# Graph layer with gathers by edge: when the dense part's work is issued, how the first groups are normalised, and how the edge list ends

## The chip, the core and the metric

The kernel runs on one core of one Trainium2 chip. A core has five engines with queues of their own: PE (TensorE, matmuls, with PEld for its weight loads), DVE (VectorE), ACT (ScalarE), POOL (GpSimd, which here issues the gathers) and SP (SyncE, which here issues the plain DMAs). The metric is the device time of the kernel in microseconds, as the median of several runs.

## What is computed

```python
def reference(x, src, dst, edge_type_4, L0_gnn_W, L0_gnn_b):   # x: 12500 x 128, 200000 edges, 4 types
    h = jnp.maximum(_layernorm(x, axis=-1), 0.0)
    xs = h[src]
    msgs = 0
    for i in range(4):
        msgs = msgs + jnp.where((edge_type_4 == i)[:, None], xs @ W[i] + b[i], 0.0)
    return x + jax.ops.segment_sum(msgs, dst, num_segments=12500)
```

The edges are sorted by destination, and the destinations are drawn so that low node numbers have many more edges than high ones.

## The kernel before

**Chunks and groups.** The edges are cut into 1,563 chunks of 128. The first 384 chunks (three blocks of 128 chunks, `DENSE = 3`) go through a dense path; the other 1,179 are handled by gathers, in groups of `G = 16` (73 groups of 16, then one of 8 and one of 3). The loop at L658 runs over these groups. For each, `gather` (L335) issues one indirect DMA on POOL for each chunk: 128 rows, one per edge, into `hm`, whose pool `rows` has five buffers of `HG = 8` chunks each. `sum_up` (L350) then makes a one-hot matrix `oh` for each chunk on DVE (L359: key equal to column number), multiplies the rows by it on PE into `ps` (L369, which sums the rows by destination and type within a window of 16, 24 or 32 nodes), copies `ps` to `sb` on ACT (L376), counts the edges by type (`pc`, L381, copied to `cnt` by L385), multiplies by the weights of the four types and adds the biases into `py` (L387, L389), and adds each chunk's window to its place in `acc`, which holds the transposed sums of all nodes in SBUF (L399, DVE). `sum_up` is a generator: it yields after each `SG = 4` chunks' copies.

**Raw groups and the table.** The first `RAW = 8` groups gather rows of `x` and normalise them after the gather (`normalize`, L294: bn_stats and bn_aggr for each row block on DVE, a square root on ACT, a reciprocal and a product on DVE, then one activation per chunk on ACT, L309). Meanwhile `table` (L311) loads `x` in pieces of `XG = 8` node columns, normalises them in the same way, splits each value into three bfloat16 parts (L318 to L321) and writes them to `htab` in HBM. From group 8 on the gathers read `htab`, three parts a row, so L369 runs three matmuls for each chunk. `prep_edges` (L190) turns blocks of 128 x 128 edges into the transposed index table `srcT` and key table `keyT`: loads of source, type and destination, DVE arithmetic, two transposes on PE through `pt`, and copies. One block is done at the head; nine more, in calls of up to four, in groups 2 to 4. `prep_dense` (L239) runs in group 1.

**The dense path.** After group 7 `make_slots` (L474) computes for the first 792 nodes a table of 984 slots (one slot: up to 128 edges of one node). `dense_work` (L597) is a generator over 18 passes of 46 columns each. A pass first builds `counts`: for each slot two one-hots on DVE (L612, L613), one matmul on PE into `pt` (L617), and a copy on ACT (L619). Then it multiplies the whole table by the counts: 98 blocks of `htab` loaded by SP in tiles `hs` of four (L627, five buffers), three matmuls a block (L633) into `pa`. `sd` takes the sum (L642), four matmuls apply the weights (L645), and the result is added to `acc` (L650). The main loop draws dense work between the parts of `sum_up`, by cost:

```python
while work and spent < share * (gi - RAW + part):     # L715
    cost = next(work, None)
```

A slot counts 0.25, a block 0.33, and `share = total / (len(sizes) - RAW - 6)`.

**The end.** `put_out` (L402) loads a piece of `x` into `xo`, transposes that part of `acc` on PE into `pt` (L416), adds (L419) and stores (L423, L425). The pieces are 8 node columns of 128 wide, and 4 among the last ones; a piece is put out as soon as no later chunk can reach it. `check_all` (L446) prepares a flag; a slow path behind it (L750) is not taken here.

**Order.** A scheduler in the framework orders each engine's instructions from the traced program, by its own model of time: an instruction traced later can stand earlier in its engine's queue where its inputs are ready earlier in that model. Each engine then runs its queue in order. PSUM pools: `x_ps` (tiles `pt`, three buffers), `s_ps` (`ps`, three), `y_ps` (`py`, one), `a_ps` (`pa`, one).

Of the kernel before, what the change touches and what calls it, by code (L numbers as in the profile page):

```python
# [32 lines left out]
F32 = mybir.dt.float32  # L33
# [10 lines left out]
P = 128  # L44
# [10 lines left out]
OB = 4  # L55
HG = 8


@with_exitstack
def kernel(  # L60
# [107 lines left out]
    wpool = whats.enter_context(tc.tile_pool(name="what", bufs=1))  # L168
    prep = early.enter_context(tc.tile_pool(name="prep", bufs=2))
    npool = early.enter_context(tc.tile_pool(name="nodes", bufs=2))  # L170


# [14 lines left out]
    nc.vector.tensor_single_scalar(span, span, 16.0, op=ALU.add)  # L187
    QB = 4

    def prep_edges(q0, q1):  # L190
        n = q1 - q0
        m0, m1 = q0 - DENSE, q1 - DENSE
        si = prep.tile([P, QB, P], I32, name="si")
        edge_rows(si, src, q0, q1, 0)
        ty = prep.tile([P, QB, P], I32, name="ty")
        edge_rows(ty, etype, q0, q1, NT)
        di = prep.tile([P, QB, P], I32, name="di")
        edge_rows(di, dst, q0, q1, 0)
# [10 lines left out]
        (nc.scalar.copy if m0 == 0 else nc.vector.tensor_copy)(srcT[:, m0:m1, :], pg[:, :n, :])  # L209
# [21 lines left out]
    nc.scalar.copy(warm, warm)  # L231
    prep_edges(DENSE, DENSE + 1)

# [49 lines left out]
    eps = const.tile([P, 1], F32, name="eps")  # L283
    nc.vector.memset(eps, EPS)
    pick = const.tile([P, NT, N3], BF16, name="pick")
# [7 lines left out]

    def normalize(xt, h, n, r, what):  # L294

        mv = what.tile([P, G, 2], F32, name="mv")
        rstd = what.tile([P, G], F32, name="rstd")
        nmr = what.tile([P, G], F32, name="nmr")
        for k in range(n):
            st = what.tile([P, 6], F32, name="st")  # L300
            nc.vector.bn_stats(st[:r], xt(k))
            nc.vector.bn_aggr(mv[:r, k, :], st[:r])
# [3 lines left out]
            nmr[:r, :n], mv[:r, :n, 0], -1.0, rstd[:r, :n], op0=ALU.mult, op1=ALU.mult  # L306
        )
        for k in range(n):
            nc.scalar.activation(h(k), xt(k), AF.Relu, bias=nmr[:r, k : k + 1], scale=rstd[:r, k : k + 1])  # L309

    def table(j0, j1, r):  # L311
        n = j1 - j0
        xt = npool.tile([P, XG, D], F32, name="xt")
        load_nodes(xt, j0, j1)
        h = npool.tile([P, XG, D], F32, name="h")
        h3 = npool.tile([P, XG, 3, D], BF16, name="h3")
        normalize(lambda k: xt[:r, k, :], lambda k: h[:r, k, :], n, r, npool)
        nc.scalar.copy(h3[:r, :n, 0, :], h[:r, :n, :])  # L318
# [30 lines left out]

    def sum_up(t0, g, rows, raw):  # L350
        win = window_of(C0 + t0)
        K = NT * win
        if raw:
            oh = npool.tile([P, G, P], F32, name="ohf")[:, :, :K]
            normalize(lambda k: rows(k, 0, 1), lambda k: rows(k, 0, 1), g, P, npool)
        else:
            oh = opool.tile([P, G, P], BF16, name="oh")[:, :, :K]
        for i in range(g):
            nc.vector.tensor_scalar(  # L359
                oh[:, i, :], (iota_f if raw else iota_b)[:, :K], keyf[:, t0 + i : t0 + i + 1], None, ALU.is_equal  # L360
            )
        sb = spool.tile([P, G * P], F32, name="sb")[:, : G * K].rearrange("p (g t n) -> p g t n", g=G, t=NT)
        nparts = 1 if raw else 3
        for i0 in range(0, g, SG):
            i1 = min(i0 + SG, g)
            ps = s_ps.tile([P, SG, P], F32, name="ps")[:, :, :K]
            for i in range(i0, i1):
                for c in range(nparts):
                    nc.tensor.matmul(  # L369
                        ps[:, i - i0, :],  # L370
# [5 lines left out]
            nc.scalar.copy(sb[:, i0:i1].rearrange("p g t n -> p g (t n)"), ps[:, : i1 - i0, :])  # L376
            yield i1 / g
        ohv = oh.rearrange("p g (t n) -> p g t n", t=NT)
# [6 lines left out]
        nc.scalar.copy(cnt[:, :g], pc[:, :g])  # L385
        py = y_ps.tile([P, G * WIN], F32, name="py")[:, : G * win].rearrange("p (g n) -> p g n", g=G)
        nc.tensor.matmul(py[:, :g, :], b12, cnt[:, :g, :], start=True, stop=False)  # L387
# [40 lines left out]
    for j0 in range(0, NW, XG):  # L428
        for ja, jb in ((j0, min(j0 + XG, NW)),) if j0 + XG < NW - XG else ((j0, j0 + XG // 2), (j0 + XG // 2, j0 + XG)):
            jb = min(jb, NW)  # L430
            if jb > ja:
                flushes.append((ja, jb, T * (min(jb * P, N) / N) ** 0.5 + ROOM - C0))

    sizes = [G] * (TM // G)
    r = TM % G
    sizes += [r - r // 3, r // 3] if r > 3 else [r] if r else []
    starts = [sum(sizes[:i]) for i in range(len(sizes))]
# [159 lines left out]
    def dense_work():  # L597
        for v0 in range(0, len(virtual), VB):
# [8 lines left out]
            for s0 in range(0, len(todo), OB):  # L607
# [6 lines left out]
                for k, (i, s, first, last) in enumerate(part):  # L614
# [3 lines left out]
                    if last:  # L618
                        nc.scalar.copy(  # L619
                            counts[:, :, i * NT : (i + 1) * NT], pb.rearrange("p (b t) -> p b t", t=NT)  # L620
                        )
                    yield 0.25
            pa = a_ps.tile([P, VB * NT], F32, name="pa")
            for j0 in range(0, NW, HB):
# [5 lines left out]
                for j in range(j0, j1):  # L630
                    r = P
                    for c in range(3):
# [6 lines left out]
                        )  # L639
                yield 0.33 * (j1 - j0)  # L640
            sd = hsp.tile([P, VB, NT], F32, name="sd")
# [16 lines left out]
    for gi, (t0, g) in enumerate(zip(starts, sizes)):  # L658
        raw = gi < RAW
        if gi == 0:  # L660
            rows = gather(t0, g, x, D)
            for a in tables[:1]:
                table(*a)
            w3 = w.rearrange("t i o -> i t o")
# [32 lines left out]
            nc.vector.tensor_copy(b12, bs)  # L697
            for a in tables[1:2]:
                table(*a)
            done = 2  # L700
        elif raw:
            rows = gather(t0, g, x, D)
            for a in tables[done : done + 2]:
                table(*a)
            done += 2
            if gi == 1:
                prep_dense()
            elif DENSE + 1 + (gi - 2) * QB < TB:
                prep_edges(DENSE + 1 + (gi - 2) * QB, min(DENSE + 1 + (gi - 1) * QB, TB))
        else:  # L710
            rows = gather(t0, g, htab, D3)
        if gi == RAW - 1:
            assert done >= len(tables)
        for part in sum_up(t0, g, rows, raw):
            while work and spent < share * (gi - RAW + part):  # L715
                cost = next(work, None)
                if cost is None:
                    work = None
                else:
                    spent += cost  # L720
        if gi == RAW - 1:
# [5 lines left out]
            whats.close()  # L727
            outp = mid.enter_context(tc.tile_pool(name="outp", bufs=2))
            dense = mid.enter_context(tc.tile_pool(name="dense", bufs=1))
# [3 lines left out]
            total = 0.25 * NS + 0.33 * NW * -(-len(virtual) // VB)  # L733
# [136 lines left out]
```

## Time and profile before

| | |
|---|---|
| median of 3 runs | 1597.66 us (1597.22 to 1600.49) |
| the profiled execution | 1600.88 us, span in the trace 1599.2 us |
| mean granted PE clock | 0.899 |
| busy: PE, DVE, ACT, POOL | 1289.5, 931.2, 621.7, 1153.8 us |
| gathers (L341) | 128 from `x`, mean 1026 ns; 1,051 from `htab`, mean 971 ns |
| one-hot pairs of the counts (L612, L613) | 984, mean 251 and 336 ns |
| products with the table (L633) | 5,292 matmuls, 469.6 us busy |
| DMA | 318.92 MB, mean 199 GB/s |

The span runs from the first to the last instruction of the trace; the profiled execution's own time is a little longer. A matmul's duration in the trace is its latency; matmuls overlap, so the distance from start to start is what a series of them costs. The same holds for DVE instructions, whose rows overlap slightly. Idle time of an engine is put down to what ended it ("issue" is time in which the profile shows nothing that the engine waited for).

### The profile page before, as it was taken

Reading aid. Unit: us, or ns where it says so; the run is one execution under the profiler, and the core shown is the slowest. Engines: PE = TensorE matmul, PEld = TensorE weight load, DVE = VectorE, ACT = ScalarE, POOL = GpSimd, SP = SyncE. Lnnn points to the kernel's source line nnn. Section 1 sums busy time; section 2 is a strip of 40 time slices with the busy share of each in tenths; the row PEclk is TensorE's granted clock in tenths of the full one; section 3 lists DMA queues with packets and bytes.
Section 4 is the critical chain, followed back from the end, with each engine's and each line's share of the span. In section 5 each row is a group of like instructions: output and inputs, shape, how many; then the busy total and the mean of one; then the engine's idle time right before and its main releaser. Section 6 shows DMA issues by size and latency. Waiting matters only on the chain.

```text
span 1599.2 us, 33065 instructions
## 1 busy us (share of the span) xinstructions
PE 1289.5 (81%) x11086; PEld 904.8 (57%) x11086; DVE 931.2 (58%) x5157; ACT 621.7 (39%) x1505; POOL 1153.8 (72%) x1189
## 2 busy tenths in 40 slices
PE   0636577888989889886589989989899889899965
PEld 0424443465757667765366766746667567486633
DVE  8786769848494573562247366564473645648232
ACT  4756723433333353251145335153252432515110
POOL 7775577277777777777767777777777777777771
PEclk9755678998989999998599999989999999999976
DMA  6453343374748759767365876848769577595641
GB/s 177 147 163 106 97 126 98 96 253 122 277 139 285 260 180 304 264 196 262 102 216 184 306 236 197 313 143 281 237 191 316 159 266 237 186 315 165 216 118 43
DMA packets 155501, 318.92 MB, mean 199 GB/s; under 512 B 28504, under 2 KB 77834, under 8 KB 155325
## 3 DMA queue, kind: packets, MB, share of 16 engines
q1 hardware_dynamic: 100781, 204.98, 36.9%
q0 software_dynamic: 54544, 111.78, 24.3%
q8 instruction: 88, 1.44, 0.4%
q14 instruction: 88, 0.72, 0.1%
HBM read 300.62 MB, written 16.03 MB: 198 GB/s over the span
## 4 chain that ended last, share of the span: by engine, by line
PE 33%; DMA 18%; DVE 15%; POOL 13%; ACT 10%; issue 8%; DVEq 0%; POOLq 0%; ACTq 0%
DMA hs<-htab 15%; PE pa L633 13%; POOL hm L341 13%; PE py L389 7%; ACT counts L619 7%; DVE o L613 6%; DVE o L612 4%; PE ps L369 4%; PE pt L617 3%; PE ps L381 2%; DVE acc L399 2%; ACT hm L309 2%; DMA hm<-htab,srcT 2%; DMA hm<-in_x_dram,srcT 1%; PE py L645 1%
## 5 line engine op out<-in xcount | busy, mean ns | idle before, releaser
L341 POOL DMA_INDIRECT hm<-htab,srcT x1051 | 1021.0, 971 | 358.9 <-issue 290.6
L633 PE MATMUL pa<-counts,hs 128*128 128x184 bf16 x5292 | 469.6, 245 | 59.5 <-DMA hs<-htab 51.5
L633 PEld LDWEIGHTS <-hs 128*128 128x128 bf16 x5292 | 416.1, 99 | 99.1 <-DMA hs<-htab 84.4
L619 ACT CAST counts<-pt 128x392 bf16<-128x392 f32 x828 | 352.1, 535 | 123.6 <-PE pt L617 119.4
L376 ACT COPY sb<-ps 128x256 f32<-128x256 f32 (+2 forms) x295 | 128.2, 445 | 637.4 <-PE ps L369 591.7
L359 DVE TENSOR_SCALAR oh<-iota_b,keyT 128x96 bf16<-128x96 bf16 (+2 forms) x1051 | 201.9, 265 | 254.8 <-PE ps L381 254.4
L399 DVE TENSOR_TENSOR acc<-acc,py 128x16 f32 (+2 forms) x1179 | 206.2, 175 | 233.3 <-PE py L389 191.0
L617 PE MATMUL pt<-o,o 128*128 128x392 bf16 x984 | 302.5, 343 | 40.0 <-DVE o L613 14.8
L613 DVE TENSOR_SCALAR o<-iota_n,hkT 128x392 bf16<-128x392 f16 x984 | 330.8, 336 | 0.0
L612 DVE TENSOR_SCALAR o<-iota_b,loT 128x128 bf16<-128x128 bf16 x984 | 247.0, 251 | 52.5 <-PE pt L617 50.1
L369 PE MATMUL ps<-oh,hm 128*128 128x96 bf16 (+2 forms) x3153 | 209.1, 207 | 64.2 <-DMA hm<-htab,srcT 57.6
L369 PEld LDWEIGHTS <-hm 128*128 128x128 bf16 x3153 | 167.2, 100 | 126.0 <-DMA hm<-htab,srcT 76.5
L389 PE MATMUL py<-sb,wsb 128*128 128x256 f32 (+2 forms) x600 | 212.3, 484 | 0.0
L617 PEld LDWEIGHTS <-o 128*128 128x128 bf16 x984 | 96.5, 100 | 186.6 <-DVE o L613 126.2
L341 POOL DMA_INDIRECT hm<-in_x_dram,srcT x128 | 131.3, 1026 | 55.2 <-issue 35.4
L389 PEld LDWEIGHTS py<-sb,wsb 128*128 128x128 f32 x600 | 115.3, 206 | 58.8 <-issue 30.9
L369 PE MATMUL ps<-ohf,hm 128*128 128x64 f32 x256 | 58.7, 416 | 92.8 <-ACT hm L309 61.9
L369 PEld LDWEIGHTS ps<-ohf,hm 128*128 128x128 f32 x256 | 54.7, 320 | 97.9 <-ACT hm L309 90.6
L385 ACT CAST cnt<-ps 12x256 bf16<-12x256 f32 (+3 forms) x75 | 31.5, 421 | 119.0 <-PE ps L381 113.6
L381 PE MATMUL ps<-oh,pick 128*12 128x384 bf16 (+3 forms) x268 | 61.4, 330 | 0.6 <-ACT sb L376 0.6
L309 ACT ACTIVATE hm<-hm,nmr,rstd 128x128 f32<-128x128 f32 x128 | 50.2, 479 | 4.9 <-DVE nmr L305 4.9
L309 ACT ACTIVATE h<-xt,nmr,rstd 128x128 f32<-128x128 f32 x98 | 40.0, 481 | 9.0 <-DVE nmr L305 9.0
(146 smaller groups left out, 522.3 us busy)
## 6 DMA issues: line engine op xcount, KB each, us to landing
hs<-htab SPq DMA_DIRECT2D x432, 384.0 KB
hm<-htab,srcT POOLq DMA_INDIRECT x1051
htab<-h SPq DMA_DIRECT2D x11, 768.0 KB
xo<-in_x_dram SPq DMA_DIRECT2D x11, 512.0 KB
out_dram<-xo SPq DMA_DIRECT2D x11, 512.0 KB
hs<-htab SPq DMA_DIRECT2D x18, 192.0 KB
xt<-in_x_dram SPq DMA_DIRECT2D x6, 512.0 KB
xt<-in_x_dram SPq DMA_DIRECT2D x5, 448.0 KB
```

Of the source, the lines that this page charges most:

```text
L309: nc.scalar.activation(h(k), xt(k), AF.Relu, bias=nmr[:r, k : k + 1], scale=rstd[:r, k : k + 1])
L341: nc.gpsimd.indirect_dma_start(out=rows[:, (i - h0) * width : (i - h0 + 1) * width], out_offset=None, in_=table, in_offset=bass.IndirectOf ...
L359: nc.vector.tensor_scalar(oh[:, i, :], (iota_f if raw else iota_b)[:, :K], keyf[:, t0 + i : t0 + i + 1], None, ALU.is_equal)
L369: nc.tensor.matmul(ps[:, i - i0, :], rows(i, c, nparts), oh[:, i, :], start=(c == 0), stop=(c == nparts - 1),)
L376: nc.scalar.copy(sb[:, i0:i1].rearrange("p g t n -> p g (t n)"), ps[:, : i1 - i0, :])
L389: nc.tensor.matmul(py[:, :g, :], wsb[:, t, :], sb[:, :g, t, :], start=False, stop=(t == NT - 1))
L399: nc.vector.tensor_tensor(to, to, py[:, i, :], ALU.add)
L612: nc.vector.tensor_scalar(o1[:, k, :], iota_b, loT[:, s : s + 1], None, ALU.is_equal)
L613: nc.vector.tensor_scalar(o2[:, k, :], iota_n, hkT[:, s : s + 1], None, ALU.is_equal)
L617: nc.tensor.matmul(pb, o1[:, k, :], o2[:, k, :], start=first, stop=last)
L619: nc.scalar.copy(counts[:, :, i * NT : (i + 1) * NT], pb.rearrange("p (b t) -> p b t", t=NT))
L633: nc.tensor.matmul(pa[:, : nv * NT], hs[:r, j - j0, c * D : (c + 1) * D], counts[:r, j, : nv * NT], start=(j == 0 and c == 0), stop=(j == ...
```

## The change

It has seven parts.

- **The dense work starts three groups later** (`LEAD = 3`: first in group 11), is spread over 60 groups instead of 61, and is costed at 0.6 for a slot and 0.3 for a block.
- **It is tied**: `sum_up` yields the last matmul of each four chunks, and `tc.issue_after(mm)` puts every PE instruction of the dense work drawn there behind that matmul in PE's queue.
- **Table statistics a group ahead**: `look` loads a piece of `x` and computes its statistics; `table`, one group later, uses them.
- **Raw groups by halves**: the one-hots come first, then each half (8 chunks) gets its own statistics and normalisation.
- **Later keys in the loop**: only two blocks are prepared in group 3; the other seven come one at a time, at groups 16, 24, ... 64, eight groups ahead of their use.
- **Smaller last groups**: 72 groups of 16, then 12, 8, 4 and 3. From group 72 on `py` is taken from `x_ps` (tiles `pt`). The last 10 node columns are put out by twos.
- `acc` is zeroed on ACT instead of DVE, and `eps` is derived from a value that depends on the first index table.

```diff
+LEAD = 3
...
-    prep = early.enter_context(tc.tile_pool(name="prep", bufs=2))
+    prep = early.enter_context(tc.tile_pool(name="prep", bufs=1))
+    aheads = early.enter_context(tc.tile_pool(name="aheads", bufs=4))
...
-    QB = 4
-    def prep_edges(q0, q1):
+    QB = max(2, DENSE)
+    def prep_edges(q0, q1, prep, QB):
...
-        (nc.scalar.copy if m0 == 0 else nc.vector.tensor_copy)(srcT[:, m0:m1, :], pg[:, :n, :])
+        nc.scalar.copy(srcT[:, m0:m1, :], pg[:, :n, :])
...
-    nc.vector.memset(eps, EPS)
+    zero = const.tile([P, 1], F32, name="zero")
+    nc.vector.tensor_single_scalar(zero, srcT[:, 0, 0:1], 0.0, op=ALU.mult)
+    nc.vector.tensor_single_scalar(eps, zero, EPS, op=ALU.add)
...
+    def look(j0, j1, r):
+        xt = npool.tile([P, XG, D], F32, name="xt", bufs=4)
+        load_nodes(xt, j0, j1)
+        seen_x[j0] = xt, stats(lambda k: xt[:r, k, :], j1 - j0, r, aheads, "t")
...
-            normalize(lambda k: rows(k, 0, 1), lambda k: rows(k, 0, 1), g, P, npool)
...
+        if raw:
+            for h0 in range(0, g, HG):
+                row = lambda k: rows(h0 + k, 0, 1)
+                n = min(HG, g - h0)
+                normalize(row, row, n, P, stats(row, n, P, npool, ""))
...
-                    nc.tensor.matmul(
+                    mm = nc.tensor.matmul(
...
-            yield i1 / g
+            yield i1 / g, mm.ins
...
-        py = y_ps.tile([P, G * WIN], F32, name="py")
+        py = (x_ps.tile([P, G * WIN], F32, name="pt") if last else y_ps.tile([P, G * WIN], F32, name="py"))
...
+        step = XG if j0 + XG < NW - XG else 2
...
+    ends_in = [12, 8, 4, 3]
+    FULL = (TM - sum(ends_in)) // G
+    r = TM - sum(ends_in) - FULL * G
+    sizes = [G] * FULL + ([r] if r else []) + ends_in
...
-                    yield 0.25
+                    yield 0.6
...
-                yield 0.33 * (j1 - j0)
+                yield 0.3 * (j1 - j0)
...
-                nc.vector.memset(acc[:, k : min(k + NC // 8, NC)], 0.0)
+                n = min(k + NC // 8, NC) - k
+                nc.scalar.copy(acc[:, k : k + n], zero.to_broadcast([P, n]))
...
-            elif DENSE + 1 + (gi - 2) * QB < TB:
-                prep_edges(DENSE + 1 + (gi - 2) * QB, min(DENSE + 1 + (gi - 1) * QB, TB))
+            elif gi == 3:
+                prep_edges(DENSE + 1, DENSE + 3, prep, QB)
...
+            q = (t0 + 8 * G) // P
+            if (t0 + 8 * G) % P < G and DENSE + 3 <= DENSE + q < TB:
+                prep_edges(DENSE + q, DENSE + q + 1, later, 1)
...
-        for part in sum_up(t0, g, rows, raw):
-            while work and spent < share * (gi - RAW + part):
+        for part, mm in sum_up(t0, g, rows, raw, gi >= FULL):
+            with tc.issue_after(mm):
+                while work and spent < share * (gi - RAW - LEAD + part):
...
-            share = total / (len(sizes) - RAW - 6)
+            share = total / (FULL - RAW - LEAD - 1)
...
-        if gi == len(sizes) - 6:
+        if gi == FULL - 6:
             check_all()
```

More of the change, by code (lines that the diff above doesn't have):

```diff
@@ L231 @@
     nc.scalar.copy(warm, warm)
-    prep_edges(DENSE, DENSE + 1)
+    prep_edges(DENSE, DENSE + 1, prep, QB)
     first0 = const.tile([P, DENSE], F32, name="first0")
@@ L291, with stats @@
     nc.vector.tensor_copy(pick_f, pick)
[L294 to L298, printed above, removed]
+    def stats(xt, n, r, what, tag):
+        mv = what.tile([P, XG, 2], F32, name="mv" + tag)
+        rstd = what.tile([P, XG], F32, name="rstd" + tag)
+        nmr = what.tile([P, XG], F32, name="nmr" + tag)
         for k in range(n):
-            st = what.tile([P, 6], F32, name="st")
+            st = what.tile([P, 6], F32, name="st", bufs=4)
             nc.vector.bn_stats(st[:r], xt(k))
@@ L307, in normalize @@
         )
+        return rstd, nmr
+    def normalize(xt, h, n, r, of):
+        rstd, nmr = of
         for k in range(n):
             nc.scalar.activation(h(k), xt(k), AF.Relu, bias=nmr[:r, k : k + 1], scale=rstd[:r, k : k + 1])
+    seen_x = {}
+    def look(j0, j1, r):
+        xt = npool.tile([P, XG, D], F32, name="xt", bufs=4)
+        load_nodes(xt, j0, j1)
+        seen_x[j0] = xt, stats(lambda k: xt[:r, k, :], j1 - j0, r, aheads, "t")
     def table(j0, j1, r):
         n = j1 - j0
-        xt = npool.tile([P, XG, D], F32, name="xt")
-        load_nodes(xt, j0, j1)
+        xt, of = seen_x.pop(j0)
         h = npool.tile([P, XG, D], F32, name="h")
         h3 = npool.tile([P, XG, 3, D], BF16, name="h3")
-        normalize(lambda k: xt[:r, k, :], lambda k: h[:r, k, :], n, r, npool)
+        normalize(lambda k: xt[:r, k, :], lambda k: h[:r, k, :], n, r, of)
         nc.scalar.copy(h3[:r, :n, 0, :], h[:r, :n, :])
@@ L348, in gather, with sum_up @@
         return lambda i, c, n: got[i // HG][:, (i % HG * n + c) * D : (i % HG * n + c + 1) * D]
-    def sum_up(t0, g, rows, raw):
+    def sum_up(t0, g, rows, raw, last):
         win = window_of(C0 + t0)
@@ L385, in sum_up @@
         nc.scalar.copy(cnt[:, :g], pc[:, :g])
-        py = y_ps.tile([P, G * WIN], F32, name="py")[:, : G * win].rearrange("p (g n) -> p g n", g=G)
+        py = (x_ps.tile([P, G * WIN], F32, name="pt") if last else y_ps.tile([P, G * WIN], F32, name="py"))[:, : G * win].rearrange("p (g n) -> p g n", g=G)
         nc.tensor.matmul(py[:, :g, :], b12, cnt[:, :g, :], start=True, stop=False)
@@ L428 @@
     for j0 in range(0, NW, XG):
[L429 to L436, printed above, removed]
+        step = XG if j0 + XG < NW - XG else 2
+        for ja in range(j0, min(j0 + XG, NW), step):
+            jb = min(ja + step, NW)
+            flushes.append((ja, jb, T * (min(jb * P, N) / N) ** 0.5 + ROOM - C0))
+    ends_in = [12, 8, 4, 3]
+    FULL = (TM - sum(ends_in)) // G
+    r = TM - sum(ends_in) - FULL * G
+    sizes = [G] * FULL + ([r] if r else []) + ends_in
     starts = [sum(sizes[:i]) for i in range(len(sizes))]
@@ L661 @@
             rows = gather(t0, g, x, D)
-            for a in tables[:1]:
-                table(*a)
+            for a in tables[:2]:
+                look(*a)
             w3 = w.rearrange("t i o -> i t o")
@@ L697 @@
             nc.vector.tensor_copy(b12, bs)
-            for a in tables[1:2]:
+            for a in tables[:2]:
                 table(*a)
+            for a in tables[2:4]:
+                look(*a)
             done = 2
@@ L704 @@
                 table(*a)
+            for a in tables[done + 2 : done + 4]:
+                look(*a)
             done += 2
@@ L707 @@
                 prep_dense()
-            elif DENSE + 1 + (gi - 2) * QB < TB:
-                prep_edges(DENSE + 1 + (gi - 2) * QB, min(DENSE + 1 + (gi - 1) * QB, TB))
+            elif gi == 3:
+                prep_edges(DENSE + 1, DENSE + 3, prep, QB)
         else:
             rows = gather(t0, g, htab, D3)
+            q = (t0 + 8 * G) // P
+            if (t0 + 8 * G) % P < G and DENSE + 3 <= DENSE + q < TB:
+                prep_edges(DENSE + q, DENSE + q + 1, later, 1)
         if gi == RAW - 1:
             assert done >= len(tables)
-        for part in sum_up(t0, g, rows, raw):
-            while work and spent < share * (gi - RAW + part):
[L716 to L720, printed above, removed]
+        for part, mm in sum_up(t0, g, rows, raw, gi >= FULL):
+            with tc.issue_after(mm):
+                while work and spent < share * (gi - RAW - LEAD + part):
+                    cost = next(work, None)
+                    if cost is None:
+                        work = None
+                    else:
+                        spent += cost
         if gi == RAW - 1:
@@ L728 @@
             outp = mid.enter_context(tc.tile_pool(name="outp", bufs=2))
+            later = mid.enter_context(tc.tile_pool(name="later", bufs=1))
             dense = mid.enter_context(tc.tile_pool(name="dense", bufs=1))
@@ L732 @@
             work = dense_work()
-            total = 0.25 * NS + 0.33 * NW * -(-len(virtual) // VB)
-            share = total / (len(sizes) - RAW - 6)
+            total = 0.6 * NS + 0.3 * NW * -(-len(virtual) // VB)
+            share = total / (FULL - RAW - LEAD - 1)
         ready = [f for f in flushes if gi >= RAW and t0 + g >= f[2] and t0 + g < TM and not (work and f[0] * P < ND)]
```

## The prediction

> **What bounds the kernel now.** I read four views: engine totals, costliest groups, the timeline of POOL's gathers, and PE's timeline around each gap in them.
>
> ```profile
> PE 1289.5 (81%) x11086; PEld 904.8 (57%) x11086; DVE 931.2 (58%) x5157; ACT 621.7 (39%) x1505; POOL 1153.8 (72%) x1189
> ...
> L341 POOL DMA_INDIRECT hm<-htab,srcT x1051 | 1021.0, 971 | 358.9 <-issue 290.6
> ...
> L341 POOL DMA_INDIRECT hm<-in_x_dram,srcT x128 | 131.3, 1026 | 55.2 <-issue 35.4 <-PE ps L369 16.2 <-ACT srcT L209 2.1
> ```
>
> POOL looks 72% busy, but it is the bound. It issues 1,179 gathers; nearly all of its idle time before the 1,051 from the table is "issue", the same 0.30 us behind every one. A gather therefore costs 0.945 + 0.305 = 1.25 us whatever the others do, 16 of them 20.0 us, and with the slower ones (39 us above 0.945 in all) 20.2 us. From the first at 4.19 to the end of the last at 1568.50 lie 1564 us; without a stop they need 1179 x 1.25 + 39 = 1513. The rest is six stops:
>
> ```profile
> 123.51 0.94 POOL L341 DMA_INDIRECT hm<-in_x_dram,srcT  x1 [1.30 <-PE ps L369]
> 153.23 0.94 POOL L341 DMA_INDIRECT hm<-in_x_dram,srcT  x1 [9.46 <-PE ps L369]
> 178.95 0.94 POOL L341 DMA_INDIRECT hm<-in_x_dram,srcT  x1 [4.57 <-PE ps L369]
> 194.43 0.94 POOL L341 DMA_INDIRECT hm<-htab,srcT  x1 [5.82 <-ACT hm L309]
> 315.29 1.28 POOL L341 DMA_INDIRECT hm<-htab,srcT  x1 [24.96 <-PE ps L369]
> 841.91 0.94 POOL L341 DMA_INDIRECT hm<-htab,srcT  x1 [8.80 <-PE ps L369]
> ```
>
> The bracket is the wait and its releaser. Above the usual 0.30 they sum to 53.1 us: 19.6 in the raw stage, 24.7 after the slot tables, 8.5 at 842. In each, all five buffers of rows (40 chunks) were full: pairing each gather with the last matmul on its chunk, POOL was 40 ahead in groups 4, 5 and 10, 35 in group 36. What PE did instead in the last two:
>
> ```profile
> 300.34 7.72 PE L617 MATMUL pt<-o,o 128*128 128x392 bf16 x22
> 307.96 0.47 PE L369 MATMUL ps<-oh,hm 128*128 128x64 bf16 x6
> ...
> 803.16 9.87 PE L617 MATMUL pt<-o,o 128*128 128x392 bf16 x26
> ...
> 815.82 5.97 PE L633 MATMUL pa<-counts,hs 128*128 128x184 bf16 x72
> ...
> 840.97 0.67 PE L369 MATMUL ps<-oh,hm 128*128 128x96 bf16 x12
> ```
>
> From 791 to 841, and from 269 to 308, PE ran one pass's counts (L617) and its products (L633) before any chunk (L369), although chunks had landed.
>
> **The raw stage.** The last chunk of raw groups 0 to 7 is consumed some 24.5 us after the last chunk of the group before (37.9 to 209.1 by group starts, seven steps), against POOL's 21. No engine is full: DVE is busy 152 of the first 200 us and ACT 126. It is a chain (gather, statistics of 16 rows, square root, 16 normalisations of 6.26 us together, matmuls). Taken out of DVE: eight memsets of `acc` (10.9 us) and seven of nine later key blocks (about 1.5 us each from L205 to L226 in the first block: 10 us). ACT gets the zeroing: L318 copies 1024 elements in 1.04 us, so 1572 in 1.6, eight 12.8; eight more half-group square roots at 0.3 add 2.4. Then DVE holds some 131 and ACT 141 us for eight groups of 21 = 168: POOL can set the pace if the waits go. The look-ahead takes bn_stats and square root out of the table's chain; the halves let statistics begin after 8 gathers, 10 us sooner. Two table tiles of rows more and one set of key buffers fewer cost no instruction. Of 19.6 us I leave 5.
>
> **Slot tables and the first dense pass.** make_slots keeps DVE from 220 to 265. POOL was never held in that time; it was held afterwards, by the first counts. With LEAD, groups 8 to 10 carry no dense work, so PE clears the backlog at about 6 us per group. Of 24.7 I leave 3, since the raw stage ends earlier and POOL meets make_slots further ahead.
>
> **Pacing and the tie.** Work is issued by cost: before 0.25 per slot and 0.33 per table block, now 0.6 and 0.3. What they take: DVE starts a one-hot pair every 0.39 us (L612 at 1441.53 and 1441.92), three products take 3 x 0.083 = 0.25 (72 in 5.97 us). One of 18 passes holds 54.7 slots and 98 blocks. Before, a group's share of 13.6 let a whole counts pass (13.7) into one group, 21 us of DVE at once; now a share is 1119.6/60 = 18.7 and the counts spread over 1.76 groups (31 slots x 0.39 = 12 of each 20.2 us) and the products over 1.58 (62 x 0.25 = 15.5). The dense chain needs 60 groups x 20.2 / 18 = 67.2 us per pass. The `sd` copies (L642) from 506 to 742 lie 59.1 us apart on average, with chunks interleaved and PE ending only 3 us behind POOL in groups 34 and 35. So it fits with 8 us per pass to spare. The tie (each dense matmul behind the last matmul of its quarter group) removes the bursts; queued behind it on PE is then dense work, while a late gather is awaited. Nearest rows for its price: 0.39 us per slot in a filled pipeline, and 1.06 us when PE waits 0.57 for ACT at each (793 to 797, where a flush held two of three `pt` buffers). I take the former; the latter would make a pass over 100 us, so the price lies between 0 and very much, and goes to the rivals. On the gain side at most the 8.5 us at 842 and what LEAD leaves. I count all 8.5.
>
> Loads: 25 tiles of 384 KB a pass, five of them prefetched, within 32 us are 241 GB/s, the gathers 79 (98 KB per 1.25 us), in sum 320. The best slices show 315 to 319 at a DMA share of 0.92. It just fits; a lag of some us is covered by the 40 chunks.
>
> [...] from 760 to 800 PE waited only about 0.9 us at a time for gathers[...] and the granted clock was
>
> ```profile
> 760.00:800.00 40.00, 20.82 (x114) 12.58 (x115) 9.81 (x55) 5.25 (x13) 30.25 (x33) 0.54 0.39 104
> ```
>
> [...] by the row a PE that has caught up runs at half speed. A quarter's 15.5 blocks then take 7.7 us of a 5.05 us slot, PE falls behind, is busy, and by the rows at 1.00 gets its clock back. I go by the row: a few us of lag per pass, under the buffers' cover, [...] as long as the lag stays below 40 chunks.
>
> **Key blocks in the loop.** Seven times 1.5 us of DVE, two transposes (0.45), two ACT copies (0.27) and three loads on SP. SP's loads stand behind `hs` loads that wait for a free buffer (760 us of such waits, 46.5 the longest), and DVE stands behind them, with one-hots and `acc` adds waiting. Cover: eight groups' lead on the keys, a lag of up to 40 chunks (50 us); without it each could stop POOL for up to some 20 us. The flushes' `xo` loads are in the same position 11 times and stop nothing. Taken at 0.
>
> **The tail.** From the start of the last gather to the end is 1599.2 - 1567.56 = 31.6 us. There `py` has one buffer: its three last users go in turn.
>
> ```profile
> 1573.13 5.24 PE L389 MATMUL py<-sb,wsb 128*128 128x512 f32 x8
> ...
> 1582.28 3.03 PE L389 MATMUL py<-sb,wsb 128*128 128x256 f32 x8
> ...
> 1587.61 2.02 PE L389 MATMUL py<-sb,wsb 128*128 128x96 f32 x8
> ...
> 1589.66 0.63 DVE L399 TENSOR_TENSOR acc<-acc,py 128x32 f32 x3 [2.37 <-PE py L389]
> ```
>
> Now 27 chunks (34 us of gathers) follow the last full group, and four groups take `py` from three buffers. What stays: landing 3.1, matmuls and counts 1.3, py 2.3, adds 0.7, four transposes for six and their adds 2.5, stores as now 6.6: 16.5. Gain 15.
>
> **Sum.** 1599.2 - 53.1 + 8 - 15 = 1539 of span; the profiled run lasted 1600.88, 1.7 more, and the median of the runs is 3.2 below that: 1537.6. One gather of 2.26 us at 19.41, under a memset that leaves DVE, may save 1. I say 1536.
>
> **Rivals.**
> 1. The start gives it back. ACT takes on 15 us, in order, at the head of a chain; the raw stops stay (+15) and the slot tables hold POOL for 12 instead of 3 (+9): 1560. For it: ACT already ends the wait at 194. Against: ACT's 141 of 168 us.
> 2. The tie does not do what it says: PE's bursts come from DVE and ACT being ahead, not from order, and two stops of together 30 us stay: 1566. Against: the chunks that PE passed over had landed.
> 3. Slower. With the dense matmuls locked in place, the round DVE, PE, ACT, PE of the counts is exposed, and PE, not POOL, sets the pace. It decides above 67.2 us per pass, and eats the gain of 62 at 67.2 + 62/18 = 70.7. At 72 it gives 1536 + 18 x 4.8 = 1622. For it: passes of 70 to 80 us exist (1106, 1302, 1375). Against: those were paced by their share, with PE 5 to 40 us behind and POOL never stopped.
>
> **Chances.** Forecast 0.62 (1522 to 1552), rival 1 0.17, rival 2 0.10, rival 3 0.09, and 0.02 that gains and losses cancel. Everything but rival 3 and the last is faster by over 0.2% (3.2 us, about what a measurement here can tell): 0.89, 0.02, 0.09. The range 1520 to 1575 holds the forecast and most of rivals 1 and 2.
>
> **What would show it.** Right: gathers at 1.25 us with stops under 12 us in sum; L617 never more than about eight in a row on PE without L369 between; `sd` copies about 67 us apart; the last gather ending near 1521; 17 us after it. Wrong: stops "<-PE ps" spread over the loop (rival 3), or a stop near 230 to 260 (rival 1); a wait of DVE for `si` or `di` with a POOL stop after it would break the zero for the key blocks.

## The result: 24.8 us faster, not 62

| | before | after |
|---|---|---|
| median, same series | 1599.08 us | 1574.32 us (1571.80 to 1575.69) |
| ratio | | 0.9835, 95% interval 0.9801 to 0.9869 |
| profiled execution, and its span | 1600.88, 1599.2 us | 1575.69, 1573.9 us |
| POOL's stops: raw groups, slots, later | 19.9, 24.7, 8.5 us | 6.3, 0, 22.5 us |
| gathers above 0.945 us, in sum | 39.0 us | 41.4 us |
| start of the last gather to the end | 31.6 us | 28.2 us |

A stop is a wait of POOL ahead of a gather, less the usual 0.30 us. The tail is counted from the start of the last gather to the end. The rows of the two spans differ by -24.3 (stops), +2.4 (slow gathers) and -3.4 (tail), together -25.3, and so do the spans. Against the forecast span of 1539 the measured one is 34.9 us too long: stops 28.8 instead of 8 (+20.8: raw groups +1.3, slots -3, later +22.5), tail 28.2 instead of 16.5 (+11.7), slow gathers +2.4. These three terms are what had to be explained.

The page of the changed kernel, engine totals and POOL's largest group (busy us and mean ns, then idle time ahead and who ended it):

```profile
PE 1290.0 (82%) x11099; PEld 906.7 (58%) x11099; DVE 914.5 (58%) x5194; ACT 632.7 (40%) x1535; POOL 1156.3 (73%) x1189
...
L357 POOL DMA_INDIRECT hm<-htab,srcT x1051 | 1028.1, 978 | 342.7 <-issue 293.2
```

PE's and POOL's totals are those of before, within 3 us; DVE has 17 us less and ACT 11 more. What has moved is the waits. Where they now are, by the timeline of POOL's gathers (start, duration, and in the bracket the wait and its releaser; the longest ones):

```profile
145.04 0.94 POOL L357 DMA_INDIRECT hm<-in_x_dram,srcT  x1 [5.70 <-PE ps L389]
957.86 1.00 POOL L357 DMA_INDIRECT hm<-htab,srcT  x1 [9.30 <-PE ps L389]
1012.67 0.94 POOL L357 DMA_INDIRECT hm<-htab,srcT  x1 [3.79 <-ACT sb L396]
1130.21 0.94 POOL L357 DMA_INDIRECT hm<-htab,srcT  x1 [6.20 <-PE ps L389]
1141.42 0.94 POOL L357 DMA_INDIRECT hm<-htab,srcT  x1 [1.52 <-PE ps L389]
1152.91 0.94 POOL L357 DMA_INDIRECT hm<-htab,srcT  x1 [1.82 <-PE pt L639]
```

The 25 us behind the slot tables and most of the raw groups' stops are gone, as forecast. In their place stand six new stops between 950 and 1340 us. Four are put down to PE's chunk matmuls (L389), one each to the copy behind them (L396) and to a count (L639). PE's timeline ahead of the longest:

```profile
894.67 0.42 PE L389 MATMUL ps<-oh,hm 128*128 128x96 bf16 x3 [0.81 <-DMA hm<-htab,srcT]
...
903.40 10.09 PE L639 MATMUL pt<-o,o 128*128 128x392 bf16 x26
...
921.89 7.11 PE L655 MATMUL pa<-counts,hs 128*128 128x184 bf16 x84
932.06 2.11 PE L655 MATMUL pa<-counts,hs 128*128 128x184 bf16 x24 [3.05 <-DMA hs<-htab]
...
955.34 0.55 PE L389 MATMUL ps<-oh,hm 128*128 128x96 bf16 x9
```

Up to 895 us PE has no chunk in arrears: it waits about 0.8 us for the rows of each. Between 904 and 955 us it takes no chunk and runs counts and products of the dense work in one stretch, as before the change ahead of the stop at 842. The tie did not remove the bursts; they come later.

The tail, by PE's weight products of the last four groups (`pt`, L409). The last gather ends at 1546.68:

```profile
1553.69 2.85 PE L409 MATMUL pt<-sb,wsb 128*128 128x384 f32 x8
...
1559.92 1.99 PE L409 MATMUL pt<-sb,wsb 128*128 128x256 f32 x8
...
1562.00 1.16 PE L409 MATMUL pt<-sb,wsb 128*128 128x128 f32 x8
...
1563.23 1.13 PE L409 MATMUL pt<-sb,wsb 128*128 128x96 f32 x8
```

The products are short: the last takes 1.13 us, where 2.3 were forecast. But the one for the group of 12 begins 7 us after the last gather, although the last chunk of that group was gathered 15 gathers (19 us) before the last gather of all.

### The profile page after: what moved, and what is told of

It reads as the page before. It is cut to its first block, busy times and chain, and to the rows that moved or that the text cites. A ratio compares the mean times of both kernels' runs of the same rounds, so it can differ in the third digit from the quotient of the medians.

```text
span 1573.9 us, 33086 instructions
## 1 busy us (share of the span) xinstructions
PE 1290.0 (82%) x11099; PEld 906.7 (58%) x11099; DVE 914.5 (58%) x5194; ACT 632.7 (40%) x1535; POOL 1156.3 (73%) x1189
## 4 chain that ended last, share of the span: by engine, by line
PE 37%; DMA 23%; DVE 17%; POOL 8%; ACT 8%; issue 6%; DVEq 0%; SPq 0%; ACTq 0%; POOLq 0%
DMA hs<-htab 20%; PE pa L655 13%; POOL hm L357 8%; PE py L409 8%; PE ps L389 5%; DVE o L635 5%; PE pt L639 4%; ACT counts L641 4%; DVE o L634 4%; PE ps L401 4%; DVE acc L419 3%; DMA hm<-htab,srcT 2%; DVE oh L374 2%; ACT hm L319 1%; PE py L407 1%
## 5 line engine op out<-in xcount | busy, mean ns | idle before, releaser
L655 PE MATMUL pa<-counts,hs 128*128 128x184 bf16 x5292 | 472.3, 245 | 80.9 <-DMA hs<-htab 72.6
L396 ACT COPY sb<-ps 128x256 f32<-128x256 f32 (+2 forms) x295 | 129.9, 448 | 570.0 <-PE ps L389 540.8
L419 DVE TENSOR_TENSOR acc<-acc,py 128x16 f32 (+2 forms) x1152 | 201.8, 175 | 232.1 <-PE py L409 218.0
L639 PE MATMUL pt<-o,o 128*128 128x392 bf16 x984 | 297.7, 346 | 29.0 <-DVE o L635 10.9
L634 DVE TENSOR_SCALAR o<-iota_b,loT 128x128 bf16<-128x128 bf16 x984 | 251.0, 255 | 116.9 <-PE pt L639 116.5
L389 PE MATMUL ps<-oh,hm 128*128 128x96 bf16 (+2 forms) x3153 | 209.0, 207 | 53.6 <-DMA hm<-htab,srcT 35.7
L389 PEld LDWEIGHTS <-hm 128*128 128x128 bf16 x3153 | 170.5, 100 | 112.1 <-DMA hm<-htab,srcT 51.9
L409 PE MATMUL py<-sb,wsb 128*128 128x256 f32 (+2 forms) x576 | 215.8, 499 | 0.0
L639 PEld LDWEIGHTS <-o 128*128 128x128 bf16 x984 | 97.3, 102 | 162.7 <-DVE o L635 84.9
L357 POOL DMA_INDIRECT hm<-in_x_dram,srcT x128 | 126.7, 990 | 47.0 <-issue 35.7
L409 PEld LDWEIGHTS py<-sb,wsb 128*128 128x128 f32 x576 | 114.9, 214 | 53.1 <-issue 26.2
L389 PE MATMUL ps<-ohf,hm 128*128 128x64 f32 x256 | 57.2, 398 | 77.2 <-ACT hm L319 35.9
L389 PEld LDWEIGHTS ps<-ohf,hm 128*128 128x128 f32 x256 | 52.3, 300 | 88.6 <-ACT hm L319 81.3
L401 PE MATMUL ps<-oh,pick 128*12 128x384 bf16 (+4 forms) x272 | 62.2, 320 | 1.8 <-ACT sb L396 1.7
L405 ACT CAST cnt<-ps 12x256 bf16<-12x256 f32 (+3 forms) x76 | 31.6, 416 | 76.4 <-PE ps L401 69.9
L664 ACT COPY sd<-pa 128x184 f32<-128x184 f32 x18 | 5.6, 312 | 108.8 <-PE pa L655 108.7
```

What stands on the lines that cost most here:

```text
L357: nc.gpsimd.indirect_dma_start(out=rows[:, (i - h0) * width : (i - h0 + 1) * width], out_offset=None, in_=table, in_offset=bass.IndirectOf ...
L389: mm = nc.tensor.matmul(ps[:, i - i0, :], rows(i, c, nparts), oh[:, i, :], start=(c == 0), stop=(c == nparts - 1),)
L401: nc.tensor.matmul(pc[:, :g, :], (pick_f if raw else pick)[:, t, :], ohv[:, :g, t, :], start=(t == 0), stop=(t == NT - 1))
L409: nc.tensor.matmul(py[:, :g, :], wsb[:, t, :], sb[:, :g, t, :], start=False, stop=(t == NT - 1))
L419: nc.vector.tensor_tensor(to, to, py[:, i, :], ALU.add)
L634: nc.vector.tensor_scalar(o1[:, k, :], iota_b, loT[:, s : s + 1], None, ALU.is_equal)
```

## The experiments

Ratios are to the kernel before in the same series, with 95% intervals; a time without a ratio is one run. In one series, with the kernels `tail_order`, `l0hs6t`, `l1hs6t` and `before_two`, the kernel before itself took 2339 us, for a cause that the profiles do not show; nothing is read from it, and the four came again as `..._b`. In the expectations a letter names a theory: F, the flushes' transposes share `pt` with the counts and push dense work behind its place in PE's queue; D, the dense chain on PE sets the loop's pace; T, PE's order in the last groups makes the tail; P, the costs give the late passes less time than PE needs.

### Is it the dense work on PE?

`no_dense` leaves the dense passes out:

```diff
-            work = dense_work()
+            work = None
```

> The changed kernel without the dense passes (counts and products of the first 384 chunks are left out; slots, gathers, chunks and flushes stay). POOL as the bound: stops only in the raw stage (about 7 us), last gather ends at 1513 to 1525, 16 to 18 us from its end to the end of the span: 1530 to 1542. If it stays above 1555, something other than the dense work holds POOL or the tail.

Measured: 1523.35 us, 7 us under the expected range; stops 2.8 us, slow gathers 17.4 instead of 41.4. So all late stops, and 24 us of slowness of the gathers themselves, come with the dense work. The tail was still 25.4 us, which no backlog of dense work can explain.

`two_parts` keeps everything but a third of the products:

```diff
-                    for c in range(3):
+                    for c in range(2):
...
-                            stop=(j == NW - 1 and c == 2),
+                            stop=(j == NW - 1 and c == 1),
```

> The changed kernel with the dense products over two of the three bf16 parts of the table: the third part is left out of the product, which takes some 8 us of TensorE's time (28 matmuls of 245 ns) off every pass and nothing else. Theory D (the dense chain on TensorE sets the loop's pace): the passes come 8 us closer where they set the pace, the stops of the gathers behind 850 us fall from 22 us to under 5, and the time is 1535 to 1552. Rival (the gathers on GpSimd set the pace and the stops come from the order of the work, not its amount): the stops stay above 15 us and the time is 1565 to 1578.

Measured: 1533.76 us, no stop behind the raw groups, 2.7 in them. POOL's waits in this kernel (in total, times, longest):

```profile
POOL hm L357 <- issue: 330.0, 1083, 0.3
...
POOL hm L357 <- PE ps L389: 4.3, 5, 3.0
```

and in the changed kernel:

```profile
POOL hm L357 <- issue: 328.9, 1079, 0.4
POOL hm L357 <- PE ps L389: 29.5, 19, 9.3
```

98 matmuls less per pass (the 28 of the expectation is a slip), some 8 us, take 40 us off: 26 of stops, and some 8 each of slow gathers and of the tail. The loads are the same, so it is PE's work that counts here. The same edit of the kernel before:

> The same kernel as before_two (the kernel before, dense products over two of three parts, the third left out), again for the same reason. Theory D (before the change TensorE's chain had room): the stops of the start and the slots stay, 1580 to 1592. Rival (it set the pace before the change as well): 1555 to 1570.

Measured: 1599.45 us, one run, beside a median of 1602.05: nothing that can be told from noise, above the expected range and on the other side of it from the rival's. Its stops at the start and behind the slots are where they were:

```profile
151.97 0.94 POOL L341 DMA_INDIRECT hm<-in_x_dram,srcT  x1 [6.04 <-PE ps L369]
177.57 0.95 POOL L341 DMA_INDIRECT hm<-in_x_dram,srcT  x1 [4.57 <-PE ps L369]
193.05 0.94 POOL L341 DMA_INDIRECT hm<-htab,srcT  x1 [5.78 <-ACT hm L309]
...
312.35 0.95 POOL L341 DMA_INDIRECT hm<-htab,srcT  x1 [22.05 <-PE ps L369]
```

The stops fell by 9.9 us in sum, 4.8 of it late in the loop, and slower gathers (+6.5) and a longer tail (+1.4) gave most of that back. So PE's dense work did not set the time before the change and does after it. That is a shift of the bound, by a change that left PE's work the same.

### Is it the order on PE?

`flush_ps` gives the flushes' transposes the chunks' pool instead of the three `pt` buffers, which they share with the counts:

```diff
-            pt = x_ps.tile([P, SG, DO], F32, name="pt")
+            pt = s_ps.tile([P, SG, DO], F32, name="ps")
```

> The changed kernel, with the flush's transposes written to a buffer of the chunks' pool (ps) instead of one of the three pt buffers. Theory F (a flush holds two of three pt buffers until acc is complete; the counts of the next pass can't start, are overdue by one to two groups, and then run as one block in front of the chunks): the six stops of POOL after 900 us (23 us in the changed kernel) fall below 5, the last gather ends near 1524 instead of 1547, and the time is 1550 to 1556. Theory C (the dense chain is too slow for 60 groups, by PE and by the loads of hs): the stops move but stay at 15 or more, and the time is 1570 to 1578.

Measured: 1610.11 us, ratio 1.0033 [1.0013, 1.0054], slower than before, and outside both expected ranges. The stops rose to 52 us in the loop. The groups of PE's instructions show a new wait in the flushes' transposes:

```profile
L436 PE MATMUL ps<-ident,acc 128*128 128x128 f32 x98 | 21.2, 384 | 53.2 <-DVE acc L419 46.5 <-DVE first L213 6.7
```

PE stood 46.5 us for DVE's additions, against 5.2 in the changed kernel. The edit brings a wait of its own, so this run alone does not settle theory F. `two_parts` above and `lead0` below do: both leave the flushes in `pt` and have no late stop. The shared buffers alone are not the cause.

`no_tie` takes the tie away:

```diff
-            with tc.issue_after(mm):
+            if True:
```

> The changed kernel without the tie; pacing and start as changed. Theory F: the tie fixes only that dense matmuls don't come early, and at the costs of 0.6 and 0.3 they rarely would; the order on PE is nearly the same, time 1574 +- 6. Theory T of the prediction (the tie removes the bursts): stops in the loop return, 1590 or more. Rival 3 of the prediction (the tie exposes the counts' round): faster, 1560 or less.

Measured: 1578.85 us, 0.9841 [0.9816, 0.9865], stops of 29.2 us. The tie does nothing that can be measured.

`keys_early` prepares all nine key blocks in groups 2 to 4, as before the change, and none in the loop:

```diff
-            elif gi == 3:
-                prep_edges(DENSE + 1, DENSE + 3, prep, QB)
+            elif DENSE + 1 + (gi - 2) * QB < TB:
+                prep_edges(DENSE + 1 + (gi - 2) * QB, min(DENSE + 1 + (gi - 1) * QB, TB), prep, QB)
...
-            if (t0 + 8 * G) % P < G and DENSE + 3 <= DENSE + q < TB:
-                prep_edges(DENSE + q, DENSE + q + 1, later, 1)
+            pass
...
```

> The changed kernel with all nine later key blocks in raw groups 2 to 4 (three each), none in the loop. Theory K (the key blocks in the loop hold pt buffers and DVE, and cause the loop's stops): the stops after 900 us fall by 15 or more and the time to 1560 or less. Theory F: the flush alone is enough to hold the counts; stops stay at 15 or more, the raw stage gets up to 8 us more, time 1570 to 1582.

Measured: 1579.31 us, 0.9818 [0.9766, 0.9870], 24.5 us of stops in the loop. The key blocks are not the cause; whether they cost a few microseconds or none can't be told.

`hs6` gives the table's blocks a sixth buffer, with `sd` cut to one to make room:

```diff
-            sd = hsp.tile([P, VB, NT], F32, name="sd")
+            sd = hsp.tile([P, VB, NT], F32, name="sd", bufs=1)
...
-            hsp = mid.enter_context(tc.tile_pool(name="hsp", bufs=5))
+            hsp = mid.enter_context(tc.tile_pool(name="hsp", bufs=6))
```

> The changed kernel with six buffers for the table's blocks instead of five (sd has one instead of two to make room). TensorE's idle time ahead of the dense products is put down to these loads for 72.6 us in the whole span. Theory D with the loads as part of the chain: half of that idle time goes and the time falls by 5 to 20 us, to 1554 to 1570. Rival (the loads wait for the program's order, what TensorE loses there it would lose elsewhere; or the single sd makes the copies wait): 1570 to 1582, with the passes still 69 us apart.

Measured: 1567.86 us, 0.9780 [0.9733, 0.9826], 20.8 us of stops in the loop. The interval overlaps that of the changed kernel: a gain of some 6 us is likely but not shown, and the late stops stay.

### Is it when the dense work starts, or how it is shared out?

`old_loop` has the changed start alone: the pacing, the dense start in group 8, the untied counts and the last groups are those of before. Of its edits:

```diff
-LEAD = 3
+LEAD = 0
...
-                    yield 0.6
+                    yield 0.25
...
-                yield 0.3 * (j1 - j0)
+                yield 0.33 * (j1 - j0)
...
```

> The kernel before with the change's start alone: statistics a group ahead, raw groups by halves, key blocks in the loop; the pacing, the place of the dense passes (from group 8), the untied counts and the last groups are those of before. Theory D: the 20 us that the raw groups are shorter move the dense start from 268 to about 248 and all passes with it, and the slots' stops stay: 1575 to 1585. Rival (the start is what the whole change brings in and pacing and tail only cost): 1555 to 1570. Rival (the pacing brings the gain, the start's time is lost in the loop): 1590 to 1602.

Measured: 1584.47 us, 0.9897 [0.9851, 0.9943]. The raw groups' stops fall to 2.3; behind the slot tables 25.4 us stay. The start alone is worth some 17 us.

`lead0` is the changed kernel with the first line of that diff alone. It also spreads the dense work over 63 groups instead of 60:

> The changed kernel with LEAD = 0: the dense passes begin at the first group after the raw ones (group 8) instead of three groups later, and their pacing is spread over 63 groups instead of 60. Theory D (the loop after the raw groups is bound by TensorE's dense chain as much as by the gathers: 18 passes of 69 us that begin at 256 us and leave their backlog to the tail): the dense work starts some 50 us earlier, near 200 us, the passes lie some 70 us apart, the last pass ends near 1480, the stops of the gathers between 850 and 1350 us (22 us now) fall to under 12, and the time is 1540 to 1560. Theory L (the lead was needed, the gathers must be some groups ahead before the dense work begins): the stops of the first passes come back, 15 to 25 us of them before 400 us, and the time is 1570 or more.

Measured: 1563.62 us, 0.9756 [0.9707, 0.9805], between the two expected ranges. No stop is left later in the loop; 8.0 us come back behind the slot tables, the most of it here:

```profile
275.41 0.95 POOL L357 DMA_INDIRECT hm<-htab,srcT  x1 [3.49 <-PE ps L389]
...
299.64 1.01 POOL L357 DMA_INDIRECT hm<-htab,srcT  x1 [4.15 <-PE ps L389]
```

In stops the lead costs more later (22.5 us) than it saves there (8.0). Of the 25.4 us that `old_loop` has behind the slots, the other changes of the loop took 17 without any lead.

What the program asks of a pass can be worked out from its costs. The 984 slots are not spread evenly: by the matmuls of L639 between two `sd` copies, the first three passes have about 92 each, the next fourteen about 46, the last 63. In the changed kernel a group's share is 1119.6 / 60 = 18.7, so a pass of 92 slots is given (92 x 0.6 + 98 x 0.3) / 18.7 = 4.53 groups, 91.6 us at 20.2 us a group, and one of 46 slots 3.05 groups, 61.7 us. `old_costs` shares out differently and keeps `LEAD = 3`:

```diff
-                    yield 0.6
+                    yield 0.25
...
-                yield 0.3 * (j1 - j0)
+                yield 0.33 * (j1 - j0)
...
-            total = 0.6 * NS + 0.3 * NW * -(-len(virtual) // VB)
+            total = 0.25 * NS + 0.33 * NW * -(-len(virtual) // VB)
```

> The changed kernel with the costs of before (0.25 per slot, 0.33 per block instead of 0.6 and 0.3); LEAD, the tie and all else as changed. By these costs a pass of 46 slots is given 43.8 of 13.8 per group, 3.18 groups (64 us), instead of 57.0 of 18.7, 3.05 groups (61.7 us); the first three passes, of 92 slots, are given 81 instead of 92 us. Theory P (the costs give the fourteen late passes less time than TensorE needs for them in the wide windows, about 66 us): the stops behind 850 us fall from 22 us to 8 to 15, some 5 us come in the first passes, the last pass ends some 15 us earlier, and the time is 1560 to 1570. Rival (the amount of dense work behind the late start alone decides, not how it is shared out): 1570 to 1580.

Measured: 1554.49 us, 0.9716 [0.9677, 0.9756], 20 us faster than the changed kernel and 6 us better than expected. The one stop over a microsecond that is left in the loop:

```profile
650.99 0.94 POOL L357 DMA_INDIRECT hm<-htab,srcT  x1 [4.19 <-PE ps L389]
```

The `sd` copies of the two kernels, first and last start, the changed kernel ahead of `old_costs`:

```profile
L664 ACT COPY sd<-pa x18: 312/312/318, 357.0 to 1531.4; 128x184 f32<-128x184 f32 x18
```

```profile
L664 ACT COPY sd<-pa x18: 312/312/313, 344.1 to 1494.6; 128x184 f32<-128x184 f32 x18
```

The third copy, which ends the long passes, lies at 541 against 508 us, the last at 1531 against 1495. The later passes take the same time in both; they only begin 33 us earlier. The last 14 distances, asked by the costs and measured, and the stops behind 335 us:

| kernel | asked, us per pass | measured | stops in the loop |
|---|---|---|---|
| before | 65.7 | 67.1 | 8.5 |
| changed | 62.5 | 65.9 | 22.5 |
| `two_parts` | 62.5 | 61.8 | 0 |
| `lead0` | 65.6 | 67.4 | 0 |
| `old_costs` | 64.6 | 66.3 | 3.9 |
| `l1_mid` (below) | 65.5 | 65.6 | 0 |

Only with 8 us less of matmuls does a pass come at 62. With all three parts they came at 65.6 to 67.4 in these five kernels. The changed kernel asks for 62.5, so that over fourteen passes the dense work falls behind by 14 x 3.4 = 48 us; some 22 of these are POOL's own stops, which hold up the groups too. What is overdue is then run in front of the chunks, and where PE is late by more than POOL's 40 chunks of room (50 us), POOL stops.

That last step is argued, not shown. The stretch without a chunk ahead of the longest stop was 52 us in the changed kernel, and the longest one behind 345 us is 25 us in `two_parts`, 41 in `lead0` and 38 in `l1_mid`, which have no late stop. But `keys_early` stops POOL for 5.6 us behind a stretch of 35, so the stretch alone does not decide it. How much is the backlog and how much its coming in one piece was not separated.

### The tail

In PE's queue the chunk matmuls of all four last groups stand ahead of the first of their `py` products. `tail_order` queues each last group's chunks behind the group before:

```diff
+                with tc.issue_after(behind[-1]) if last and behind else nullcontext():
...
+        if last:
+            behind.append(pm.ins)
```

(`pm` is the last matmul of L409.)

> The same kernel as tail_order (chunk matmuls of the last groups queued behind the py products of the group before), again, because in the series before this one the kernel before took 2339 us instead of 1600. Theory T: the tail behind the last gather shrinks from 27 to 17 to 21 us: 1564 to 1569. Rival (the backlog of the dense passes makes the tail): 25 to 28 us, 1570 to 1578.

Measured: 1575.04 us, 0.9847 [0.9816, 0.9878]: no gain in the median. In the profiled execution the tail was 23.5 us from the start of the last gather instead of 28.2, but the product of the group of 12 still began at 1543.08, half a microsecond before the last gather's end: PE took the last chunk of group 71 18 us after it had been gathered. Order and backlog both hold it, so the order alone isn't enough. `l0hs6t` joins it to `LEAD = 0` and the sixth buffer:

> The same kernel as l0hs6t (LEAD = 0, six buffers for the table's blocks, the order of the last groups), again for the same reason. Theory D with T: 1548 to 1557. Rival (the three act on the same wait): 1560 to 1566.

Measured: 1553.28 us, 0.9699 [0.9669, 0.9728], as expected; tail 20.1 us against 28.5 for `lead0`, with 8.2 us of stops behind the slots. That the backlog alone is not to blame either is seen in `old_costs`. Its last `sd` copy lies 27 us ahead of the last gather, and PE has caught up so far that it waits for each gather. Yet the product of the group of 12, whose last chunk PE had taken by 1507, comes behind the last chunk of all, and the tail is 28.6 us:

```profile
1524.89 0.50 PE L389 MATMUL ps<-oh,hm 128*128 128x128 bf16 x3 [1.25 <-DMA hm<-htab,srcT]
...
1527.88 3.35 PE L409 MATMUL pt<-sb,wsb 128*128 128x384 f32 x8
```

In `two_parts` the scheduler itself put this product ahead of the last five chunks (1509.61, the last chunk at 1515), and the tail was 20.5 us without the new order.

### Together

`l1hs6t` is `l0hs6t` with `LEAD = 1`, and `l1_mid` has that with 0.4 per slot and 0.3 per block.

> The same kernel as l1hs6t (LEAD = 1, six buffers, the order of the last groups), again for the same reason as the two before. With LEAD = 0 this gave 1553 with 8.2 us of stops behind the slots and passes of 46 slots paced at 64.8 us. Theory P: LEAD = 1 paces them at 63.8 us; the slots' stops go (8 us) and 3 to 10 us of stops come in late passes: 1547 to 1558. Rival (the dense start alone sets the end): 1565 to 1575.

> As l1hs6t with the costs 0.4 per slot and 0.3 per block: passes of 46 slots are paced at 64.9 us, those of 92 at 89. Theory P: both the slots' stops and those of the late passes are small (together under 8 us): 1543 to 1553. Rival (the dense start alone sets the end): 1565 to 1575.

Measured: `l1hs6t` 1541.86 us, 0.9640 [0.9597, 0.9684]; `l1_mid` 1541.23 us, 0.9616 [0.9579, 0.9653]. Both are below their expected ranges and beat both kernels. In `l1_mid` POOL is the bound as the forecast had it; its waits:

```profile
POOL hm L357 <- issue: 331.2, 1087, 0.3
POOL hm L357 <- PE ps L392: 7.7, 12, 4.3
```

and the end of its timeline, where the product of the group of 12 runs under the last gathers:

```profile
1517.08 4.06 PE L412 MATMUL pt<-sb,wsb 128*128 128x384 f32 x8
...
1522.66 0.95 POOL L357 DMA_INDIRECT hm<-htab,srcT  x1 [0.30 <-issue]
...
1530.99 1.13 PE L412 MATMUL pt<-sb,wsb 128*128 128x96 f32 x8
```

Its last gather ends at 1523.6, where the prediction has it near 1521, and 17.9 us follow.

## Why the prediction was right and wrong

**Right: what bounded the kernel before, and the first two terms.** POOL's stops were the loss, and PE's dense work did not set the time: `before_two_b` gained nothing. The raw groups' stops fell from 19.9 to 6.3 (forecast 5; its 19.6 for before is a slip, as its lines give 19.9), the slots' from 24.7 to 0 (forecast 3), with the start alone (`old_loop`) worth some 17 us in time. So rival 1, that the start gives it back, did not come. At the slots the prediction credits the lead; `lead0` shows that without it only 8 of the 25 us stay, and with `LEAD = 1` (`l1hs6t`) none. The three groups it took were not priced: `lead0` is faster than the changed kernel by 0.8% of the time before, though the intervals just overlap.

**Wrong, the largest term (20.8 us in the stops, 22.5 of it later in the loop): "it fits with 8 us per pass to spare".** The step took 60 groups over 18 passes, 67.2 us, as what each pass is given, and compared it with 59.1 us, the distance of passes 4 to 7 of before. Both sides were off. The passes are not equal: by the costs, which were in the diff, three get 91.6 us and the fourteen that decide get 61.7. The lines showed it, too: in the stretch from 269 to 308 us of before, where the prediction saw counts and products of one pass, PE ran some 92 counts, and the products began behind it. And 59.1 was measured where the groups' windows are 16 wide; from group 35 on they are 24. There `py` products take 2.85 us a group instead of 1.99, and a group's 48 chunk matmuls follow each other every 42 ns instead of 29 (both in the changed kernel), which makes some 5 us a pass by an estimate from these numbers. Over the last fourteen passes before the change the same view showed 67.1. So there was nothing to spare, and the late stops, put at 0, came to 22.5 us. The costs of 0.6 and 0.3 are what turned it into a loss: taken back alone, with the lead kept (`old_costs`), they are worth 20 us.

It is the place of rival 3 (PE sets the pace), with another mechanism than the one given there: not the round DVE, PE, ACT, PE that the tie exposes, since without the tie (`no_tie`) nothing changes. The clock, which the prediction read as half speed from its row at 0.54, did not enter: in the changed kernel it was granted at 0.98 from 609 to 1500 us.

**Wrong: "the tie removes the bursts".** L639 still runs up to 38 in a row without a chunk between, not eight. Rival 2 said so, and its 30 us of stops are near the measured 28.8, though they lie later than it placed them, so the number is luck in part. Its reason, DVE and ACT being ahead, was not tested.

**Wrong, the second term (11.7 us): the tail of 16.5.** The products in that sum were no longer than forecast. What failed is the assumption that only the group of 3 is left when its rows land. PE's queue held the chunks of all last groups ahead of the product of the group of 12, and the backlog held both. With the order and the backlog mended the tail is 18.8 us (`l1_mid`); `tail_order_b` and `old_costs` show that neither alone does it.

**Right: loads and key blocks at 0, as far as the runs can tell.** `keys_early` gained nothing, `hs6` at most a few microseconds. The slow gathers, put at their 39 us of before, were right within 2.4 us. With the pacing and the tail mended, a lead of 1 and the sixth buffer (`l1_mid`), the forecast of 1536 is missed by 5 us.

What stays open: why a late pass takes about 66 us when PE is busy 787 of 891 us between 609 and 1500 (a part of the rest is waits for `hs`, 72.6 us in the whole span); why PE's order puts a whole pass in front of the chunks; and how much of the sixth buffer's gain is real.

## What to carry to other kernels

When work is spread by a cost model, work out what each unit is given from the costs themselves and compare it with the slowest stretch of the trace, not an average with the fastest. A change that removes waits on the bounding engine can use up the room of the next one: here 8 us less of PE's work per pass was worth nothing before and 40 us after. And a tail shortened on paper is only short if the engine's queue has it in that order and nothing is left over in front of it.

## What the runs showed of the hardware

How far instructions overlap in the trace, before the change: the 72 products (L633) behind 815.82 us took 239 to 253 ns each but 5.97 us together, 83 ns for each; in the one-hot pairs (L612, L613) behind 1441.53 us the two took 0.25 and 0.32 us, and a pair began every 0.39 us.

A gather's own time changed with what ran beside it: above 0.945 us each, the 1,179 gathers took 41.4 us in sum with the dense work and 17.4 without it. Which part of the dense work does it, DVE's one-hots or the loads of `hs`, was not separated.

PE's granted clock was lower in stretches where PE had caught up. In the prediction's row it was 0.54, with PE's waits for gathers at 0.27 to 1.03 us each and one of 2.22; from 840 to 880 us, with PE busy 38.5 of the 40 us, it was 1.00. In `no_dense`, from 1400 to 1490 us, it was 0.66 (columns: window, its length, busy us of PE, PEld, DVE, ACT and POOL, granted clock, DMA share, GB/s):

```profile
1400.00:1490.00 90.00, 60.84 (x276) 28.46 (x274) 20.58 (x139) 12.73 (x22) 68.04 (x73) 0.66 0.34 89
```

In `old_costs` it was 0.72 from 1522 to 1545, in the changed kernel, with its backlog, 1.00 from 1546 to 1567. PE's products of the last four groups took 9.1 us together in the one (3.35, 2.69, 1.97, 1.13) and 7.1 in the other (2.85, 1.99, 1.16, 1.13). So having caught up ahead of the tail went with 2 us more in the tail's matmuls.
